# A decoder layer in fp32 on one core: the first entry's order written out on four engines, the identity made first, loads reordered, and the experts' sums taken in another order

## The chip, the core and the metric

One core of a Trainium2 chip runs the whole layer as one program. The metric is the time of the program on the device in microseconds, as a median of several executions. A core has five engines with a queue of instructions each: PE (TensorE, matrix products and transposes), DVE (VectorE), ACT (ScalarE), POOL (GpSimd) and SP (SyncE, which here only issues DMAs). ACT and POOL issue DMAs too. An engine takes its queue in order, so an instruction that waits holds up all that stands behind it.

## The reference

What is computed, cut to what matters (16 entries of 128 tokens, 256 wide):

```python
x = x + attn(layernorm(x))             # 16 heads of 64, self-attention within an entry
x = x + xattn(layernorm(x), ctx, mask) # 16 heads of 16, keys and values from ctx, keys masked
x = x + ffn(layernorm(x))              # all 8 experts, 256 -> 512 -> 256, exact gelu, summed,
                                       # times norm_g = g / (g + 1e-6) of the top gate
...
logits = xf @ gate_w.T + gate_b
logits = logits * rsqrt(mean(logits ** 2) + eps) * rms_w
g = softmax(logits / 0.5).max(-1)
```

Every expert's output counts for every token; the gate only gives the factor.

## The kernel before, in words

**Loads** (lines 130 to 198). SP and ACT issue the big loads, POOL the small ones: the row constants `rowv` broadcast to all partitions, the mask `msk`, and eight column pieces `bqk2`. SP starts with the first entry's tokens and shares the four quarters of `wq` and `wk` with ACT; ACT then issues the two halves of `wv`, SP the tokens of entries 1 to 3 in one load, the first context, the cross-attention's weights `wx` (in small pieces) and `wx_vo`, the remaining tokens, `wo`, and the experts' first weights. A load's landing is told by one of eight semaphores in turn, so a ninth load is issued when the first has landed.

**The identity** (lines 201 and 202) is written by POOL, two operations; PE's transposes multiply by it.

**The entry of token block 0** (lines 786 to 825). Statistics and inverse root on DVE (`deviations`, lines 250 to 291), the normalized tokens `xn` (295), two transposes on PE (304), a copy by ACT to `xnT` (246 or 234, both are helpers through which many operations pass), keys and queries (378, four columns of heads per call: `keys(0, 0)`, `queries(0, 0)`, ...), values (417), then the same normalization for block 1. Around it stand preparations: the scaled bias `bk1` (205), the statistics of blocks 2 and 3, `hidden_keys` from the mask (803), `masked`, `par` and `bkp` (805 to 819) for the cross-attention, and two cleared tiles `v2` (824). In this stretch only PE's order is that of the code; the order on DVE, ACT and POOL is chosen by a scheduler when the program is built.

**The slots** (lines 737 to 784, 827 to 835). After the entry, 16 slots run, one per entry, in which self-attention of entry s, cross-attention of s-1 and s-2, the expert norm of s-3 and the projections of s+1 are woven together. Each step has a due time in the table `DUE` (in us of a slot of 28.2); `at` puts it in a heap, `run_slots` takes the steps out in order of due time, and that order holds on PE, DVE, ACT and POOL. Slot 0 starts with the scores S0 and S1 (433). Then follow the largest value per row `nmax` (319), exponentials (325, ACT), reciprocals `rinv` (336), the product with them on POOL (340), transposes `tr_p` (355), their copies `prT` by DVE, the products `po` with the values (457), `atT`, and the output product `mm_o` (477), which reads `wo`. Twelve late statistics `st0` to `st11` are spread over slot 0.

**The experts** (lines 982 to 1121). Four blocks of 512 tokens; the products of 2x2 blocks are done with seven products in place of eight. For each of 16 pairs p of hidden blocks: four products into the banks ha, hb, hf, he (`hidden_first`), three more added into ha, hf, he (`hidden_last`), gelu on ACT, and seven products into sums 1 to 7 (`summed`). The sums lie two to a PSUM bank in the order `ORDER = (2, 3, 4, 8, 1, 7, 5, 6)`, so the banks hold (2, 3), (4, 8), (1, 7) and (5, 6). At the end of a token block `finished` combines the sums: ACT copies sum 1 to `u[0]`, DVE adds (1036 to 1042) and writes `yT` with the bias (`plus`, 1032). While the next block runs its pairs 0 and 1 this goes on; after pair 1, `rest` transposes yT on PE (eight transposes, banks hb and hf), DVE multiplies by the gate and adds the tokens (`ot`, 1055), and SP stores. Here only PE's order is written; ACT's and DVE's is the scheduler's.

Of the kernel before, what the change touches and what calls it, by code (L numbers as in the profile page):

```python
# [18 lines left out]
P = 128  # L19
# [7 lines left out]
C2 = 2  # L27
# [37 lines left out]
    cmul1b=27.42, lg=27.6, xn3=27.77, cke=28.26, ab2=28.44, st0=14.3, st1=14.8, st2=15.6,  # L65
    st3=16.2, st4=17.4, st5=17.9, st6=18.4, st7=18.9, st8=20.0, st9=20.5, st10=21.0, st11=21.5,
    late=31.7,
# [6 lines left out]
def decoder_layer(  # L74
# [21 lines left out]

    const = ctx.enter_context(tc.tile_pool(name="const", bufs=1))
# [21 lines left out]


# [16 lines left out]
    for n in range(4):  # L137
        for w, src, q in ((wq, wq1, nc.sync), (wk, wk1, nc.scalar)):
            f = slice(n * 256, (n + 1) * 256)
            q.dma_start(out=w[:, :, f], in_=src[:, :, f])  # L140
    for n in range(2):
        f = slice(n * 512, (n + 1) * 512)
        nc.scalar.dma_start(out=wv[:, :, f], in_=wv1[:, :, f])
    load_tokens(1, 3)
# [21 lines left out]
    wx_vo = wx_p.tile([P, 2, KD, D], F32, tag="wx_vo", name="wx_vo")  # L166
    for n, w in ((1, wk2), (0, wq2)):
        for k in range(KD):
            nc.sync.dma_start(
                out=wx[:, n, k].rearrange("p (h d) -> p h d", d=DH2),  # L170
                in_=w[:, k].rearrange("p (h s) -> p h s", s=32)[:, :, :DH2],
            )
    nc.sync.dma_start(out=wx_vo[:, 0], in_=wv2)
# [27 lines left out]
    ident = const.tile([P, P], F32, tag="ident", name="ident")  # L201
    make_identity(nc, ident)

    bk1 = const.tile([P, C1], F32, tag="bk1", name="bk1")
    nc.vector.tensor_scalar_mul(bk1, colv[:, BK1 : BK1 + C1], DH1 ** -0.5)
# [531 lines left out]
    def slot(s):  # L737
# [38 lines left out]
        if s == 0:  # L776
            mv = variances(B - 4)
# [8 lines left out]
    with tc.manual_schedule(engines={mybir.EngineType.PE}):  # L786
        first = deviations([0])
        self_norm(0)
        add_bias(0, BO1)
        self_norm_transposed(0)  # L790
        first.update(deviations([1]))
        self_norm(1)
        add_bias(1, BO1)
        for n in range(2):
            keys(0, n)
            queries(0, n)
        values(0, 0)
        self_norm_transposed(1)
        values(0, 1)
        first.update(deviations([2, 3]))  # L800

        hidden_keys = const.tile([P, T], U8, tag="hidden_keys", name="hidden_keys")
        nc.vector.tensor_scalar(hidden_keys, msk, 0, None, ALU.is_equal)
        masked = const.tile([P, 1], F32, tag="masked", name="masked")
        nc.vector.memset(masked, MASKED)


        par = const.tile([P, 2], F32, tag="par", name="par")
        bkp = const.tile([P, 2, C2], F32, tag="bkp", name="bkp")
# [11 lines left out]
        v2s = []  # L821
        for i in range(2):
            v2 = wx_p.tile([P, GB, 2 * VW], F32, tag=f"v2_{i}", name=f"v2_{i}")
            nc.gpsimd.memset(v2, 0.0)
            v2s.append(v2)

    with tc.manual_schedule(
        engines={
            mybir.EngineType.PE,
            mybir.EngineType.DVE,  # L830
            mybir.EngineType.Activation,
            mybir.EngineType.Pool,
        }
    ):
        run_slots(B)
# [190 lines left out]
    def finished(m, sums, plain):  # L1026
# [7 lines left out]
        nc.scalar.copy(u[:, 0], ys[1])  # L1034
        plus(yT[:, 0, :HT], 0, ys[2], u[:, 0])
        nc.vector.tensor_add(u[:, 1], u[:, 0], ys[6])
        nc.vector.tensor_add(u[:, 3], u[:, 1], ys[5])
        plus(yT[:, 0, HT:], 0, ys[3], u[:, 3])
        nc.vector.tensor_add(u[:, 2], u[:, 1], ys[7])  # L1039
        plus(yT[:, 1, :HT], 1, ys[4], u[:, 2])  # L1040
        if plain:
            nc.vector.tensor_add(u[:, 2], u[:, 2], ys[8])
        plus(yT[:, 1, HT:], 1, ys[5], u[:, 2])

        def rest():
            for i in range(MT // P // 2):
                tr = ps_h.tile([P, 4, P], F32, tag=("hb", "hf")[i], name="tr_y")
                for j in range(2):
                    for k in range(KD):
                        t0 = (2 * i + j) * P  # L1050
                        nc.tensor.transpose(tr[:, 2 * j + k, :], yT[:, k, t0 : t0 + P], ident)
                ot = rp.tile([P, 2, D], F32, tag="ot", name="ot")
                b0 = m * (MT // P) + 2 * i
                for j in range(2):
                    nc.vector.scalar_tensor_tensor(
                        ot[:, j, :],
                        tr[:, 2 * j : 2 * j + 2, :].rearrange("p k t -> p (k t)"),
                        gn[:, b0 + j : b0 + j + 1],
                        xs[:, b0 + j, :],
                        ALU.mult,  # L1060
                        ALU.add,
                    )
                nc.sync.dma_start(
                    out=out[b0 : b0 + 2].rearrange("b t d -> t b d"), in_=ot
                )

# [13 lines left out]
    def experts():  # L1080
# [12 lines left out]
        for m in range(NT // MT):  # L1093
            for p in range(0 if m else PRE, NP):
# [20 lines left out]
                if p == 1 and rest is not None:  # L1115
                    rest()
                    rest = None
# [71 lines left out]
```

## Time and profile before

| what | us |
|---|---|
| median of 3 executions (lowest, highest) | 886.25 (886.09, 886.84) |
| the profiled execution, its span | 886.86, 884.9 |
| PE busy in the span | 860.6 |
| first transpose, first product of keys, first scores | 12.72, 14.79, 28.69 |
| start of the scores of slots 1, 2, 3 | 51.40, 75.57, 103.36 |
| joints of the experts' token blocks (first product of the next block's sums) | 584.13, 683.75, 783.41 |
| last product of the sums, last store issued | 877.50, 881.81 |

Times count from the start of the span. A row of the timeline has start, duration, engine, line, operation, what it writes `<-` what it reads, how many were merged, and in brackets how long the engine had been idle and what ended that. A row of the waits has the engine and line that waited, for whom, the total, the number of times and the longest.

### The profile page before, as it was taken

Reading aid. Unit: us, or ns where it says so; the run is one execution under the profiler, and the core shown is the slowest. Engines: PE = TensorE matmul, PEld = TensorE weight load, DVE = VectorE, ACT = ScalarE, POOL = GpSimd, SP = SyncE. Lnnn points to the kernel's source line nnn. Section 1 sums busy time; section 2 is a strip of 40 time slices with the busy share of each in tenths; the row PEclk is TensorE's granted clock in tenths of the full one; section 3 lists DMA queues with packets and bytes.
Section 4 is the critical chain, followed back from the end, with each engine's and each line's share of the span. In section 5 each row is a group of like instructions: output and inputs, shape, how many; then the busy total and the mean of one; then the engine's idle time right before and its main releaser. Section 6 shows DMA issues by size and latency. Waiting matters only on the chain.

```text
span 884.9 us, 16050 instructions
## 1 busy us (share of the span) xinstructions
PE 860.6 (97%) x5984; PEld 721.3 (82%) x5984; DVE 626.4 (71%) x1528; ACT 425.8 (48%) x1622; POOL 166.3 (19%) x178
## 2 busy tenths in 40 slices
PE   3999999999999999999999999999999999999997
PEld 3788888888888888888876558878888888878886
DVE  3687877778777877778776489675657666575655
ACT  1457655675557655675544804333333333333332
POOL 3224232342334232342322100000000000000000
PEclk9999999999999999999999999999999999999999
DMA  9700000000000000000051010000000000000000
GB/s 211 258 1 13 2 2 13 1 13 1 1 14 1 14 1 1 14 1 1 2 183 56 1 49 0 1 24 1 1 0 1 25 1 1 0 24 1 1 1 24
DMA packets 19262, 21.30 MB, mean 24 GB/s; under 512 B 9504, under 2 KB 15664, under 8 KB 18544
## 3 DMA queue, kind: packets, MB, share of 16 engines
q1 hardware_dynamic: 17040, 17.84, 6.4%
q10 hardware_dynamic: 1776, 2.14, 0.9%
q8 instruction: 47, 0.77, 0.4%
q0 software_dynamic: 368, 0.30, 0.3%
q14 instruction: 31, 0.25, 0.1%
HBM read 18.16 MB, written 2.10 MB: 23 GB/s over the span
## 4 chain that ended last, share of the span: by engine, by line
PE 91%; DVE 5%; ACT 1%; DMA 1%; issue 1%; POOL 0%; SPq 0%; ACTq 0%; DVEq 0%; POOLq 0%
PE y L980 18%; PE mm_qk L378 13%; PE mm_v L417 6%; PE tr_p L355 6%; PE mm_o L477 6%; PE hf L980 5%; PE he L980 5%; PE ha L980 5%; PE sc L433 3%; PE po L457 3%; PE y L867 3%; PE hb L980 3%; PE mm_h L727 3%; PE sc L567 2%; PE po L606 2%; PE mm_k L494 2%
## 5 line engine op out<-in xcount | busy, mean ns | idle before, releaser
L340 POOL TENSOR_TENSOR cpr<-cpr,rinv 128x512 f32<-128x512 f32 x64 | 68.5, 1070 | 221.5 <-DVE rinv L336 221.1
L325 ACT ACTIVATE cpr<-sc,nmax 128x128 f32<-128x128 f32 x256 | 89.7, 411 | 11.6 <-DVE nmax L319 11.6
L325 ACT ACTIVATE pr<-sc,nmax 128x128 f32<-128x128 f32 x256 | 90.6, 419 | 1.8 <-DVE nmax L319 1.8
L319 DVE TENSOR_REDUCE nmax<-sc 128x8 f32<-128x1024 f32 x64 | 76.7, 1219 | 10.7 <-PE sc L433 10.7
L340 POOL TENSOR_TENSOR pr<-pr,rinv 128x512 f32<-128x512 f32 x64 | 65.9, 1041 | 80.8 <-DVE rinv L336 80.8
L1010 DVE TENSOR_TENSOR c<-u,hf 128x256 f32<-128x256 f32 x56 | 23.6, 421 | 71.7 <-PE hf L980 71.6
L1009 ACT ACTIVATE h<-u,colv 128x256 f32<-128x256 f32 x56 | 28.4, 507 | 91.9 <-DVE u L996 90.2
L378 PEld LDWEIGHTS mm_qk<-xnT,wk 128*128 128x128 f32 x512 | 62.5, 196 | 8.9 <-issue 4.3
L246 ACT COPY xnT<-tr_x 128x256 f32<-128x256 f32 x42 | 15.6, 372 | 109.9 <-PE tr_x L304 109.9
L980 PE MATMUL hf<-xt,w 128*128 128x256 f32 x224 | 67.1, 381 | 0.3
L980 PE MATMUL ha<-xnT,w 128*128 128x256 f32 x224 | 66.6, 379 | 0.0
L980 PE MATMUL y<-t,w 128*128 128x256 f32 x224 | 66.6, 379 | 0.0
L325 ACT ACTIVATION_READ_ACCUMULATOR pr<-sc,nmax 128x1 f32 x256 | 66.3, 259 | 0.0
L378 PE MATMUL mm_qk<-xnT,wk 128*128 128x128 f32 x512 | 64.2, 280 | 1.4 <-ACT xnT L234 1.4
L378 PE MATMUL mm_qk<-xnT,wq 128*128 128x128 f32 x512 | 65.1, 281 | 0.0
L325 ACT ACTIVATION_READ_ACCUMULATOR cpr<-sc,nmax 128x1 f32 x256 | 64.4, 252 | 0.0
L378 PEld LDWEIGHTS mm_qk<-xnT,wq 128*128 128x128 f32 x512 | 61.1, 195 | 3.0 <-issue 2.9
L993 ACT COPY u<-ha 128x256 f32<-128x256 f32 x56 | 20.8, 372 | 87.1 <-PE ha L980 87.1
L417 PE MATMUL mm_v<-wv,xnT 128*128 128x512 f32 x128 | 60.2, 592 | 0.0
L980 PE MATMUL y<-h,w 128*128 128x256 f32 x224 | 57.7, 380 | 1.4 <-DVE yu L1039 1.4
L477 PE MATMUL mm_o<-wo,atT 128*128 128x256 f32 x256 | 57.9, 379 | 0.0
L246 DVE COPY prT<-tr_p 128x512 f32<-128x512 f32 x64 | 39.8, 684 | 19.4 <-PE tr_p L355 19.3
(164 smaller groups left out, 1880.2 us busy)
## 6 DMA issues: line engine op xcount, KB each, us to landing
w<-in_w SPq DMA_DIRECT2D x8, 1024.0 KB, 5.4
ctx<-in_ctxT SPq DMA_DIRECT2D x8, 256.0 KB, 2.7
out_x<-ot SPq DMA_DIRECT2D x8, 256.0 KB, 2.2
xs<-in_x SPq DMA_DIRECT2D x3, 512.0 KB, 7.0
wk<-in_wk ACTq DMA_DIRECT2D x4, 256.0 KB, 9.2
wq<-in_wq SPq DMA_DIRECT2D x4, 256.0 KB, 10.6
wv<-in_wv ACTq DMA_DIRECT2D x2, 512.0 KB, 7.9
wo<-in_wo SPq DMA_DIRECT2D x1, 1024.0 KB, 9.9
```

The lines of the kernel that those rows point to most:

```text
L246: f(*a)
L319: nc.vector.tensor_reduce(w["nmax"], sc, AX.X, ALU.max, negate=True)
L325: nc.scalar.activation(w["pr"][:, i, :], sc[:, i, :], AF.Exp, bias=w["nmax"][:, i : i + 1], scale=1.0, accum_out=sums[:, j : j + 1],)
L340: nc.gpsimd.tensor_tensor(four, four, w["rinv", n].unsqueeze(2).broadcast_to([P, 4, T]), ALU.mult)
L355: nc.tensor.transpose(tr[:, j, :], w["pr"][:, 4 * n + j, :], ident)
L378: nc.tensor.matmul(mm[:, i, :], w[:, k, c * P : (c + 1) * P], xnT1[:, k, 0, :], start=(k == 0), stop=(k == KD - 1),)
L417: nc.tensor.matmul(mm, entry["xnT1", b][:, k, 0, :], wv[:, k, f], start=(k == 0), stop=(k == KD - 1),)
L433: nc.tensor.matmul(sc[:, j, c * T : (c + 1) * T], qT[r, 4 * half + c, :], kT[r, 4 * half + c, :], start=True, stop=True,)
L457: nc.tensor.matmul(po[j * DH1 : (j + 1) * DH1, c, :], v[:, h * DH1 : (h + 1) * DH1], prT[:, 4 * j + c, :], start=True, stop=True,)
L477: nc.tensor.matmul(mm[:, :D], atT[:, c, :], wo[:, c, :], start=(c == 0), stop=(c == C1 - 1))
L980: nc.tensor.matmul(out, left[p // q][n - 1][:, p % q], rights[n - 1], **flags)
L1009: nc.scalar.activation(h[:, 1, 1], u[:, 3], AF.Gelu, bias=col(B1 + 2 * p + 1))
```

## The change

- One written order for PE, DVE, ACT and POOL from the beginning of the program to the end of the slots, in place of PE's alone in the entry.
- The identity is made ahead of all loads.
- Loads: wv's halves go from ACT's queue to SP's, behind the tokens of entry 1, which are loaded alone; the cross-attention's value weights (`wx_vo[:, 0]`) and the tokens of entries 2 and 3 go ahead of `wx`.
- `bk1` stands behind the first normalization; the statistics of block 1 stand behind the first keys and queries; those of blocks 2 and 3 become steps of slot 0 (due 6.65, 6.7 and 7.9), and the masks' and biases' preparation becomes a step of slot 0 (`cross`, due 13.9). The cleared tiles v2 go ahead of the entry.
- Experts: `finished` adds in another order (`u[2]` right after `u[1]`, all three ahead of the outputs; the two outputs of the second half exchanged where `plain` is not set); `rest` is done in two portions, after pairs 1 and 2, both through the bank he; the last pair's products come in the order 1, 5, 7, 6, 2, 3, 4.

```diff
-    cmul1b=27.42, lg=27.6, xn3=27.77, cke=28.26, ab2=28.44, st0=14.3, st1=14.8, st2=15.6,
+    cmul1b=27.42, lg=27.6, xn3=27.77, cke=28.26, ab2=28.44, early0=6.65, early1=6.7, early=7.9,
+    cross=13.9, st0=14.3, st1=14.8, st2=15.6, st3=16.2, st4=17.4, st5=17.9, st6=18.4, st7=18.9,
...
+    in_order = ExitStack()
+    in_order.enter_context(
+        tc.manual_schedule(
+            engines={
+                mybir.EngineType.PE,
+                mybir.EngineType.DVE,
+                mybir.EngineType.Activation,
+                mybir.EngineType.Pool,
+            }
+        )
+    )
...
+    ident = const.tile([P, P], F32, tag="ident", name="ident")
+    make_identity(nc, ident)
...
+    load_tokens(1, 1)
     for n in range(2):
         f = slice(n * 512, (n + 1) * 512)
-        nc.scalar.dma_start(out=wv[:, :, f], in_=wv1[:, :, f])
-    load_tokens(1, 3)
+        nc.sync.dma_start(out=wv[:, :, f], in_=wv1[:, :, f])
...
+    nc.sync.dma_start(out=wx_vo[:, 0], in_=wv2)
+    load_tokens(2, 2)
     for n, w in ((1, wk2), (0, wq2)):
...
-    nc.sync.dma_start(out=wx_vo[:, 0], in_=wv2)
...
-    ident = const.tile([P, P], F32, tag="ident", name="ident")
-    make_identity(nc, ident)
...
-    nc.vector.tensor_scalar_mul(bk1, colv[:, BK1 : BK1 + C1], DH1 ** -0.5)
...
         if s == 0:
+            mv2 = variances(2)
+            for i in range(2):
+                at(f"early{i}", statistics, mv2[:, i, :], 2 + i)
+            at("early", lambda: first.update(inverse_deviations(mv2, [2, 3])))
+            at("cross", for_cross)
...
+    first = deviations([0])
+    self_norm(0)
+    add_bias(0, BO1)
+    self_norm_transposed(0)
+
+    nc.vector.tensor_scalar_mul(bk1, colv[:, BK1 : BK1 + C1], DH1 ** -0.5)
+    keys(0, 0)
+    queries(0, 0)
+    first.update(deviations([1]))
+    self_norm(1)
+    add_bias(1, BO1)
+    keys(0, 1)
+    queries(0, 1)
+    values(0, 0)
+    self_norm_transposed(1)
+    values(0, 1)
...
         nc.scalar.copy(u[:, 0], ys[1])
+        nc.vector.tensor_add(u[:, 1], u[:, 0], ys[6])
+        nc.vector.tensor_add(u[:, 2], u[:, 1], ys[7])
+        nc.vector.tensor_add(u[:, 3], u[:, 1], ys[5])
         plus(yT[:, 0, :HT], 0, ys[2], u[:, 0])
-        nc.vector.tensor_add(u[:, 1], u[:, 0], ys[6])
-        nc.vector.tensor_add(u[:, 3], u[:, 1], ys[5])
         plus(yT[:, 0, HT:], 0, ys[3], u[:, 3])
-        nc.vector.tensor_add(u[:, 2], u[:, 1], ys[7])
-        plus(yT[:, 1, :HT], 1, ys[4], u[:, 2])
         if plain:
+            plus(yT[:, 1, :HT], 1, ys[4], u[:, 2])
             nc.vector.tensor_add(u[:, 2], u[:, 2], ys[8])
-        plus(yT[:, 1, HT:], 1, ys[5], u[:, 2])
+            plus(yT[:, 1, HT:], 1, ys[5], u[:, 2])
+        else:
+            plus(yT[:, 1, HT:], 1, ys[5], u[:, 2])
+            plus(yT[:, 1, :HT], 1, ys[4], u[:, 2])
...
-                tr = ps_h.tile([P, 4, P], F32, tag=("hb", "hf")[i], name="tr_y")
+            tr = ps_h.tile([P, 4, P], F32, tag=bank, name="tr_y")
...
-                if p == 1 and rest is not None:
-                    rest()
-                    rest = None
+                if p in (1, 2) and rest is not None:
+                    rest(p - 1, "he")
                 before = now
-        summed((1, 2, 3), *before, ys)
-        summed((7, 5, 6, 4), *before, ys)
-        finished(m, ys, False)()
+        summed((1, 5, 7, 6, 2, 3, 4), *before, ys)
+        rest = finished(m, ys, False)
+        for i, bank in enumerate(("hb", "hf")):
+            rest(i, bank)
```

The function `for_cross` holds what stood at lines 803 to 819, unchanged.

More of the change, by code (lines that the diff above doesn't have):

```diff
@@ L64 @@
     root=24.79, k1=25.19, ve1=25.39, gate=26.93, ke1=27.13, cr1b=27.14, ck=27.19, xn=27.27,
-    cmul1b=27.42, lg=27.6, xn3=27.77, cke=28.26, ab2=28.44, st0=14.3, st1=14.8, st2=15.6,
-    st3=16.2, st4=17.4, st5=17.9, st6=18.4, st7=18.9, st8=20.0, st9=20.5, st10=21.0, st11=21.5,
-    late=31.7,
+    cmul1b=27.42, lg=27.6, xn3=27.77, cke=28.26, ab2=28.44, early0=6.65, early1=6.7, early=7.9,
+    cross=13.9, st0=14.3, st1=14.8, st2=15.6, st3=16.2, st4=17.4, st5=17.9, st6=18.4, st7=18.9,
+    st8=20.0, st9=20.5, st10=21.0, st11=21.5, late=31.7,
 )
@@ L784, in slot, with for_cross @@
             at("late", rest)
[L786 to L802, printed above, removed]
+    v2s = []
+    for i in range(2):
+        v2 = wx_p.tile([P, GB, 2 * VW], F32, tag=f"v2_{i}", name=f"v2_{i}")
+        nc.gpsimd.memset(v2, 0.0)
+        v2s.append(v2)
+    first = deviations([0])
[13 more added lines that the diff above has]
+    values(0, 1)
+    hidden_keys = const.tile([P, T], U8, tag="hidden_keys", name="hidden_keys")
+    masked = const.tile([P, 1], F32, tag="masked", name="masked")
+    par = const.tile([P, 2], F32, tag="par", name="par")
+    bkp = const.tile([P, 2, C2], F32, tag="bkp", name="bkp")
+    def for_cross():
         nc.vector.tensor_scalar(hidden_keys, msk, 0, None, ALU.is_equal)
-        masked = const.tile([P, 1], F32, tag="masked", name="masked")
         nc.vector.memset(masked, MASKED)
-        par = const.tile([P, 2], F32, tag="par", name="par")
-        bkp = const.tile([P, 2, C2], F32, tag="bkp", name="bkp")
         for e in range(2):
@@ L819, in decoder_layer @@
             nc.vector.tensor_scalar_mul(bkp[:, e, :], bqk2[:, 1, :], par[:, e : e + 1])
[L821 to L835, printed above, removed]
+    run_slots(B)
+    in_order.close()
     alone.close()
@@ L1041, in finished @@
         if plain:
+            plus(yT[:, 1, :HT], 1, ys[4], u[:, 2])
             nc.vector.tensor_add(u[:, 2], u[:, 2], ys[8])
-        plus(yT[:, 1, HT:], 1, ys[5], u[:, 2])
-        def rest():
-            for i in range(MT // P // 2):
-                tr = ps_h.tile([P, 4, P], F32, tag=("hb", "hf")[i], name="tr_y")
[L1048 to L1064, printed above, removed]
+            plus(yT[:, 1, HT:], 1, ys[5], u[:, 2])
+        else:
+            plus(yT[:, 1, HT:], 1, ys[5], u[:, 2])
+            plus(yT[:, 1, :HT], 1, ys[4], u[:, 2])
@@ new lines, in rest @@
+        def rest(i, bank):
+            tr = ps_h.tile([P, 4, P], F32, tag=bank, name="tr_y")
+            for j in range(2):
+                for k in range(KD):
+                    t0 = (2 * i + j) * P
+                    nc.tensor.transpose(tr[:, 2 * j + k, :], yT[:, k, t0 : t0 + P], ident)
+            ot = rp.tile([P, 2, D], F32, tag="ot", name="ot")
+            b0 = m * (MT // P) + 2 * i
+            for j in range(2):
+                nc.vector.scalar_tensor_tensor(
+                    ot[:, j, :],
+                    tr[:, 2 * j : 2 * j + 2, :].rearrange("p k t -> p (k t)"),
+                    gn[:, b0 + j : b0 + j + 1],
+                    xs[:, b0 + j, :],
+                    ALU.mult,
+                    ALU.add,
@@ L1065, in rest @@
                 )
+            nc.sync.dma_start(out=out[b0 : b0 + 2].rearrange("b t d -> t b d"), in_=ot)
         return rest
```

## The prediction

> **What bounds the kernel now.** I read the page first, then who TensorE (PE) waited for, then the timeline of the stages that the diff touches. The page:
>
> ```profile
> PE 860.6 (97%) x5984; PEld 721.3 (82%) x5984; DVE 626.4 (71%) x1528; ACT 425.8 (48%) x1622; POOL 166.3 (19%) x178
> PE 91%; DVE 5%; ACT 1%; DMA 1%; issue 1%; POOL 0%; SPq 0%; ACTq 0%; DVEq 0%; POOLq 0%
> ```
>
> PE is busy for 97% of the span and 91% of the chain that ended last is PE. The change takes no arithmetic away, so it can only gain where PE stands still. PE's waits, longest first (total, times, longest):
>
> ```profile
> PE tr_x L304 <- POOL ident masks.py:199: 12.7, 1, 12.7
> PE tr_y L1051 <- DVE yT L1032: 1.5, 1, 1.5
> PE hb L980 <- DVE ot L1055: 1.5, 3, 0.5
> PE y L980 <- DVE yu L1039: 1.4, 3, 0.5
> PE mm_qk L378 <- ACT xnT L234: 1.4, 1, 1.4
> ```
>
> The first and the last are the entry, about 14 us; the three in between are the three joints of the experts' token blocks and the tail, about 4 us. So the entry decides. Its timeline:
>
> ```profile
> 1.27 0.74 POOL L145 DMA_DIRECT2D rowv<-in_rows  x1 [0.82 <-POOLq L1177]
> ...
> 4.16 0.15 DVE L255 TENSOR_SCALAR root_t<-var 128x1 int32<-128x1 int32 x1
> ...
> 9.16 3.87 ACTq L143 DMA_DIRECT2D wv<-in_wv  x2
> ...
> 9.54 0.23 DVE L803 TENSOR_SCALAR hidden_keys<-msk 128x128 uint8<-128x128 uint8 x1 [5.23 <-DMA msk<-in_mask]
> ...
> 11.21 0.41 DVE L295 TENSOR_SCALAR xn<-xs,mv,root 128x256 f32<-128x256 f32 x1
> ...
> 12.38 0.29 POOL masks.py:199 TENSOR_SCALAR_AFFINE_SELECT ident<-ident 128x128 f32<-128x128 f32 x1
> ...
> 13.07 1.28 ACT L234 ACT_TABLE_LOAD   x1 [13.07 <-DMA wk<-in_wk]
> 14.36 0.37 ACT L234 COPY xnT<-tr_x 128x256 f32<-128x256 f32 x1
> ...
> 14.79 3.78 PE L378 MATMUL mm_qk<-xnT,wk 128*128 128x128 f32 x16 [1.37 <-ACT xnT L234]
> ```
>
> The reader is to see three queues blocked by something that the first product does not need: DVE stands 5.23 us behind hidden_keys, which waits for the mask; POOL writes the identity behind its own loads; ACT issues the two halves of wv (each issue waits for an earlier load) before its table load and the copy.
>
> **1. The entry.** In the built order of the changed kernel hidden_keys is gone from before xn, the identity is POOL's first work, and ACT issues only colv and wk.
> - DVE: after root_t (end 4.31) the rest of the chain, 9.69 to 11.62 in the trace, is 1.93 us: xn ends at 6.3.
> - POOL: free at 1.27; 0.22 and 0.29 us of row time, and at most the 1.08 us that POOL idled between them: identity by 2.9. Hidden behind xn; without that cover it would cost what passes 6.3.
> - PE's two transposes take 0.69 us: 7.1. ACT is through with its issues at 4.55, the table load ends near 5.9, the copy takes 0.37: 7.5.
> - The first product also needs the first quarter of wk. By its issue (1.19) and landing time (8.0 us) that landed at 9.2; the other quarters, in the same way: wk 10.0, 12.6, 14.2; wq 9.3, 12.4, 13.9, 14.9.
>
> So the first product starts between 7.5 (data early) and 9.2 (data as before). What held the data? Columns here: stretch, busy per engine, clock, share of DMA time, GB/s.
>
> ```profile
> 4.00:6.00 2.00, 0.00 (x0) 0.00 (x0) 0.28 (x2) 0.00 (x0) 2.00 (x4) 1.00 0.75 153
> 6.00:8.00 2.00, 0.00 (x0) 0.00 (x0) 0.00 (x0) 0.00 (x0) 0.21 (x1) 1.00 1.03 336
> ```
>
> Until rowv has landed (1.27 + 6.9 = 8.2) the rate is half of what it is afterwards. rowv is now issued 0.5 to 1.6 us later, behind the identity, so some of wk and wq gets past it. I take the middle, **8.3: 6.5 us earlier** than 14.79 (ends 5.6 and 7.3).
>
> From there I move the old sequence as it is. Eight matmuls of a quarter take 8 x 0.213 = 1.7 us at first, so the quarters are wanted at 8.3, 10.0, 11.7, 13.4 and on, no earlier than they landed. wv is wanted at 8.3 + 10.15 = 18.5 and 20.4; it landed at 17.8 and 19.6 with 384 KB of tokens beside it, and now has 128 KB ahead of it. The context and wv2 are wanted at 24.2 and come right after wv, 512 KB, 1.7 us at 300 GB/s. SP's queue also carries tokens 2 and 3 ahead of wx now: first used in slot 0, near 28. wo is wanted near 37.8 and landed at 35.2, with the same bytes ahead of it: 2.6 us of cover.
>
> The clock: mm_qk starts are 0.213 us apart until 20.9 and 0.112 after, 6.1 us from the first product, though the clock column says 1.00. I keep that stretch as long as it was.
>
> [...]
>
> **2. What moves into slot 0.** DVE had the roots of tokens 2 and 3 and the masks' constants behind it before the scores; now they stand in slot 0. In the trace's own times:
>
> ```profile
> 35.76 0.18 DVE L336 RECIPROCAL rinv<-sums 128x4 f32<-128x4 f32 x1 [1.22 <-ACT pr L325]
> ...
> 37.16 0.18 DVE L336 RECIPROCAL rinv<-sums 128x4 f32<-128x4 f32 x1 [1.22 <-ACT pr L325]
> 37.25 0.38 DVE L295 TENSOR_SCALAR xn<-xs,mv,root 128x256 f32<-128x256 f32 x1
> 37.41 1.12 POOL L340 TENSOR_TENSOR pr<-pr,rinv 128x512 f32<-128x512 f32 x1 [0.36 <-DVE rinv L336]
> 37.57 2.68 DVE L246 COPY prT<-tr_p 128x512 f32<-128x512 f32 x4
> ```
>
> The four statistics (1.1 us, as the pair at 40.17 to 41.25) fit in the idle before 35.76. The twelve root operations do not: the same twelve for 12 columns run from 54.80 to 57.15, 2.3 us. They stand between the third and the fourth reciprocal, so the fourth goes from 37.16 to 38.2, the fourth product on POOL ends at 39.5 instead of 38.53, and the four prT copies end near 41.1 instead of 40.25. PE's second po group starts right after them (40.48): **0.9 us later**. Queued behind it on DVE are the masks' constants (about 1.2 us) and the late statistics; atT then ends at 44.0 and 45.7, wanted at 44.3 and 46.0: covered, by 0.3 us. In slot 1 nmax starts 0.4 later than PE's own shift, which that slot's transposes just absorb. Ends: 0.3 (POOL's product was late only by the overlap) and 1.8 (the cover of 0.3 is gone in slots 0 and 1).
>
> **3. The joints, three times.** Before:
>
> ```profile
> 584.13 1.10 PE L980 MATMUL y<-h,w 128*128 128x256 f32 x4 [0.52 <-DVE yu L1039]
> ...
> 589.74 1.65 DVE L1055 SCALAR_TENSOR_TENSOR ot<-tr_y,gn,xs 128x256 f32<-128x256 f32 x4
> ...
> 590.76 0.67 PE L980 MATMUL hb<-xt,k 128*128 128x256 f32 x2 [0.49 <-DVE ot L1055]
> ```
>
> - Transposes in two portions. PE's products come 0.43 us apart; hb came at 590.76 instead of 590.1 and hf then at 591.54 instead of 591.19: 1.0 us lost. Now four transposes stand ahead of ha, and the bank is he, wanted as the fourth product, near 590.53; two ot end at 590.6. About 0.23 us lost, twice: 0.55 saved per joint, **1.6 us** in three (ends 0.6 and 2.4).
> - Order of the sums. Product 1 wants the bank of sums 1 and 7, freed by yu (L1039): a place earlier now, 0.33 us. But in the built DVE order (left to the scheduler) another yT stands ahead of the one that frees the bank of sums 2 and 3; that ends at 584.8 instead of 584.4, and product 2 starts at 584.93 instead of 584.56. So 0.37 us is lost per joint, of which the first gets 0.18 back at he, where PE waited for DVE anyway: **+0.9 us** (ends -1.0, if the bank comes free in time, and +1.1).
>
> **4. The tail.** Sum 7 is the third product instead of the fourth, so the copy of sum 1 starts 0.43 earlier (876.25). But DVE then has three yu and four yT in a row: 876.68 + 0.46 + 0.33 + 0.33 + 3 x 0.42 + 0.48 = 879.54, where the yT that PE waited for ended at 879.46. **+0.1** (ends -0.4, +0.4).
>
> **Sum.** -6.5 + 0.9 - 1.6 + 0.9 + 0.1 = -6.2. The profiled execution took 886.86 with a span of 884.9, 2.0 around it: 878.7 + 2.0 = **880.7**. Its own time is 0.6 above the median of the three (886.25, from 886.09 to 886.84), the high end of them.
>
> **Rivals.**
> - The data set the start (25%): wk lands at 9.2 as before, and the slot-0 loss is at its upper end. -5.6 + 1.8 - 0.6 = -4.4, or **882.5**. For it: landing times show no slack below 9.2. Against: rowv is out of the way at first.
> - The data come early (17%): start at 7.5, and the bank of sums 2 and 3 is free in time. -7.3 + 0.9 - 1.6 - 1.0 + 0.1 = -8.9, **878.0**.
> - wv goes through one queue instead of two (5%): both queues were in use until wv landed, and if SP's queue alone is slower, wv, the context and wo slide. values(0,0) would wait; with the gain cut to within 1.7 us, about **885.5**. Against: SP alone carries 254 to 415 GB/s from 24 to 38.
> - wo is too late, and slower than before (3%): the output product of slot 0 stands behind it. It costs from a landing at 37.8 on; from 44 the whole gain is gone, from 46 it is slower: at 48, **888.7**. It would have to land 13 us later than it did with the same bytes ahead, hence the small chance.
>
> Forecast 50%. Faster by over 0.2% (1.77 us, about what a measurement of this kernel can tell from no change): 50 + 25 + 17 = 92%; within 5%; slower 3%. The range leaves out the last two and the outer half of the early case: 878.2 to 883.6.
>
> **What would show it.** PE's wait for the identity is gone and tr_x starts near 6.4; the first mm_qk starts at 7.5 to 9.2 and waits for a load; the first sc starts near 22.2 instead of 28.69; a PE gap of about a microsecond appears at tr_p or po in slot 0; hb's wait is gone and he waits 0.2 us six times; y at the joints waits for yT rather than yu. I am wrong if the first mm_qk starts after 10, if mm_v or mm_o waits for a load, or if slots 1 to 3 take longer than before.

## The result

The changed kernel takes **879.6 us** (median of 6 executions, 878.69 to 882.39); the kernel before, run beside it, 886.17 us (6 executions, 885.25 to 886.84). The ratio is 0.9928, with a 95% interval from 0.9913 to 0.9944. A second series later, on another chip, gave 880.31 us (5 executions, 879.63 to 882.20) against 886.02 us, ratio 0.9945 [0.9932, 0.9959]. Forecast: 880.7, range 878.2 to 883.6.

The profiled execution of the changed kernel took 879.95 us, its span is 878.2. Its page, the same two lines as before (busy time of the engines, and the chain that ended last):

```profile
PE 859.7 (98%) x5984; PEld 719.8 (82%) x5984; DVE 626.4 (71%) x1528; ACT 426.1 (49%) x1622; POOL 166.6 (19%) x178
...
PE 92%; DVE 4%; issue 1%; DMA 1%; ACT 1%; POOL 0%; DVEq 0%; ACTq 0%; POOLq 0%
```

The instructions are as many as before, 5984 matmuls and 1528 operations of DVE, and DVE's busy time is the same; PE's is 0.9 us less, although it does the same products. That 0.9 is a first hint that the clock had a part in it. What PE waited for (total, times, longest):

```profile
PE tr_x L315 <- DVE bk L814: 6.2, 1, 6.2
PE mm_qk L389 <- DMA wk<-in_wk: 1.9, 1, 1.9
PE tr_p L366 <- POOL pr L351: 1.5, 1, 1.5
PE tr_y L1066 <- DVE yT L1045: 1.3, 2, 0.8
PE y L993 <- DVE yT L1045: 1.2, 3, 0.4
...
PE he L993 <- DVE u L1009: 0.2, 1, 0.2
```

Of the five waits of before, hb's is gone and the first is half as long. The first product waits for a load now. The third row is new: 1.5 us in slot 0 for a product of POOL. The entry, from the timeline:

```profile
1.02 0.29 POOL masks.py:199 TENSOR_SCALAR_AFFINE_SELECT ident<-ident 128x128 f32<-128x128 f32 x1
...
1.46 0.74 POOL L159 DMA_DIRECT2D rowv<-in_rows  x1 [0.15 <-issue]
...
4.27 1.28 ACT L245 ACT_TABLE_LOAD   x1 [4.27 <-issue]
...
5.65 0.41 DVE L306 TENSOR_SCALAR xn<-xs,mv,root 128x256 f32<-128x256 f32 x1
...
6.21 0.66 PE L315 MATMUL tr_x<-ident,xn 128*128 128x128 f32 x2 [6.21 <-DVE bk L814]
6.90 0.37 ACT L245 COPY xnT<-tr_x 128x256 f32<-128x256 f32 x1 [1.35 <-PE tr_x L315]
...
8.76 0.55 PE L389 MATMUL mm_qk<-xnT,wk 128*128 128x128 f32 x1 [1.90 <-DMA wk<-in_wk]
```

The identity is ready at 1.3, xn at 6.1, the copy at 7.3; then PE stands 1.90 us until the first quarter of wk is there. (The first row of the waits names `bk`, which follows xn on DVE; the transposes wait for xn.)

The two profiled executions, mark by mark, in us from the start of the span:

| mark | before | after | gained so far |
|---|---|---|---|
| first transpose | 12.72 | 6.21 | 6.5 |
| first product of keys | 14.79 | 8.76 | 6.02 |
| first scores (slot 0) | 28.69 | 21.29 | 7.40 |
| scores of slot 1 | 51.33 | 45.59 | 5.74 |
| scores of slot 3 | 103.29 | 97.67 | 5.62 |
| first product of the experts | 526.33 | 520.47 | 5.86 |
| last product of the sums | 877.51 | 870.40 | 7.11 |
| end of the span | 884.88 | 878.18 | 6.70 |

So 6.02 come from the start, 1.38 more until the scores, 1.66 are lost in slot 0, 1.25 come back at the joints, and 0.41 is lost after the last product.

### The profile page after: what moved, and what is told of

Same layout as the page of the kernel before. It is cut to its first block, busy times and chain, and to the rows that moved or that the text cites. A ratio compares the mean times of both kernels' runs of the same rounds, so it can differ in the third digit from the quotient of the medians.

```text
span 878.2 us, 16053 instructions
## 1 busy us (share of the span) xinstructions
PE 859.7 (98%) x5984; PEld 719.8 (82%) x5984; DVE 626.4 (71%) x1528; ACT 426.1 (49%) x1622; POOL 166.6 (19%) x178
## 4 chain that ended last, share of the span: by engine, by line
PE 92%; DVE 4%; issue 1%; DMA 1%; ACT 1%; POOL 0%; DVEq 0%; ACTq 0%; POOLq 0%
PE y L993 18%; PE mm_qk L389 13%; PE mm_v L428 6%; PE tr_p L366 6%; PE mm_o L488 6%; PE he L993 5%; PE hf L993 5%; PE ha L993 5%; PE sc L444 4%; PE po L468 3%; PE y L880 3%; PE mm_h L738 3%; PE hb L993 3%; PE sc L578 2%; PE po L617 2%; PE mm_k L505 2%
```

## The experiments

Twelve experiments. Each starts from the changed kernel; times of a single execution are so marked. The span marks are those of the table above. Experiments 1 to 4 ran on one chip, 5 to 8 on another, 9 to 12 on a third, each beside the kernel before (medians 885.49, 885.68 and 886.02 us), so small differences are read from stretches of a profile and not from the whole time.

**1. wv back on ACT's queue.**

```diff
-        nc.sync.dma_start(out=wv[:, :, f], in_=wv1[:, :, f])
+        nc.scalar.dma_start(out=wv[:, :, f], in_=wv1[:, :, f])
```

> The changed kernel with one of its three repairs undone: wv's two loads are issued by ACT again, behind wk. Theory (each of the three queues held the start by itself): ACT's two issues wait for earlier loads and end near 10.3 us, the table load (1.28) and the copy (0.37) follow, so the first mm_qk starts near 12.1 instead of 8.76, and the time is 3.3 us longer. Rival (the other two repairs carry the gain, and ACT's queue was in nobody's way): first mm_qk within 0.5 us of 8.76.

Measured (one execution): 888.19 us, span 886.3. The first product starts at 14.12, later than even the theory had it, for ACT's two issues lasted longer. The timeline of ACT, and the product:

```profile
8.16 4.21 ACTq L158 DMA_DIRECT2D wv<-in_wv  x2
12.40 1.28 ACT L245 ACT_TABLE_LOAD   x1 [12.40 <-DMA wk<-in_wk]
13.70 0.37 ACT L245 COPY xnT<-tr_x 128x256 f32<-128x256 f32 x1
...
14.12 1.22 PE L389 MATMUL mm_qk<-xnT,wk 128*128 128x128 f32 x4 [7.26 <-ACT xnT L245]
```

This one line of the change undone takes back 5.36 of the 6.02 us. The time is 2.7 us above the kernel before beside it, although only the start was touched: against the changed kernel the span is 8.1 us longer, of which 5.36 come from the first product, 1.2 from the stretch up to the scores and 1.6 from slot 0. The last two are a matter of the clock (below).

**2. The identity behind POOL's loads again.**

```diff
-    ident = const.tile([P, P], F32, tag="ident", name="ident")
-    make_identity(nc, ident)
...
+    ident = const.tile([P, P], F32, tag="ident", name="ident")
+    make_identity(nc, ident)
     bk1 = const.tile([P, C1], F32, tag="bk1", name="bk1")
```

> The changed kernel with the identity behind POOL's own loads again. Theory: POOL comes to it near 10.8 us, it is done near 11.4, transposes 0.66, copy 0.37: first mm_qk near 12.5, 3.7 us later than in the changed kernel, and as much longer in time. Rival: no loss over 0.5 us.

Measured (one execution): 883.17 us. Identity written from 9.67 to 10.26, first transpose 10.32, first product 11.47: 2.7 us later, a microsecond less than the theory said.

```profile
9.97 0.29 POOL masks.py:199 TENSOR_SCALAR_AFFINE_SELECT ident<-ident 128x128 f32<-128x128 f32 x1
...
10.32 0.69 PE L315 MATMUL tr_x<-ident,xn 128*128 128x128 f32 x2 [10.32 <-POOL ident masks.py:199]
```

**3. hidden_keys ahead of the first normalization again.**

```diff
+    nc.vector.tensor_scalar(hidden_keys, msk, 0, None, ALU.is_equal)
     first = deviations([0])
```

> The changed kernel with hidden_keys ahead of the first statistics on DVE. Theory: DVE stands until the mask has landed (near 10.2 us), then its chain of 3.0 us, transposes and copy follow: first mm_qk near 14.6, 5.9 us later than in the changed kernel. Rival: no loss over 0.5 us, because the data were what the start waited for.

Measured (one execution): 884.75 us. hidden_keys at 9.43, first transpose 12.72, first product 13.84: 5.1 us later, 0.8 less than the theory said.

```profile
9.43 0.23 DVE L810 TENSOR_SCALAR hidden_keys<-msk 128x128 uint8<-128x128 uint8 x1 [6.04 <-DMA msk<-in_mask]
```

The three parts undone one at a time cost 5.4, 2.7 and 5.1 us, 13.2 together, where all together brought 6.0. They lie side by side on three engines: ACT's queue or DVE's alone holds PE nearly as long as all three, the identity alone for less than half of it.

**4. The roots of tokens 2 and 3 back in the entry**, and their load ahead of the context.

```diff
-            at("early", lambda: first.update(inverse_deviations(mv2, [2, 3])))
...
     values(0, 1)
+    first.update(deviations([2, 3]))
```

> The changed kernel with the statistics and roots of tokens 2 and 3 taken out of slot 0 and put at the end of the entry, and their load put ahead of the first context. Theory (the roots in slot 0 cost PE its gap of 1.5 us at tr_p): tokens 2 and 3 land near 18.5 us, the roots end near 22, before the first nmax at 22.5; the gap at tr_p goes to under 0.3, slot 0 (scores to scores of slot 1) goes from 24.3 to 22.7 us, and the time is 1.3 to 1.6 us shorter than that of the changed kernel (879.6), so 878.0 to 878.3. Rival (the gap comes from POOL's or ACT's own pace there, which was there before in small): the gap stays over 1 us and the time is the same within 0.3.

Measured: median 878.96 us (4 executions, 878.25 to 879.87), ratio to before 0.9920 [0.9904, 0.9937]. The theory's 878.0 to 878.3 us is missed by 0.7, and a gain over the changed kernel (ratio 0.9928) is not shown by the whole times. The slot shows it: slot 0 lasts 22.59 us instead of 24.30 (before: 22.64). In its stretch the waits of PE hold only

```profile
PE tr_p L366 <- ACT kT L415: 0.3, 1, 0.3
```

The 1.5 us for POOL's product are gone. The roots ended at 23.33 and not near 22, still 0.6 us ahead of the first nmax (23.95). The scores start 1.45 us later than in the changed kernel; the clock came up at 14.96, 6.10 us behind the first product instead of 3.27, and half of that difference is 1.4.

**5. The roots one place earlier in slot 0**: `early=7.8` instead of 7.9.

> The roots of token tiles 2 and 3 stand one place earlier in slot 0: ahead of the third reciprocal instead of behind it; nothing else differs from the changed kernel. [...] Slot 0 24.3 us long, to 0.3. [...]

What it is to tell apart is seen in the changed kernel's slot 0: whether the 1.05 us of one operation come from POOL's product beside it or from the operation's own form.

```profile
28.47 0.14 DVE L294 TENSOR_SCALAR var<-mv 128x2 f32<-128x2 f32 x1
...
28.63 1.04 POOL L351 TENSOR_TENSOR pr<-pr,rinv 128x512 f32<-128x512 f32 x1 [0.36 <-DVE var L294]
28.64 1.05 DVE L266 TENSOR_SCALAR root_t<-var 128x2 int32<-128x2 int32 x1
...
29.73 0.17 DVE L267 TENSOR_SCALAR root<-root_t 128x2 int32<-128x2 int32 x1
...
31.57 0.17 DVE L347 RECIPROCAL rinv<-sums 128x4 f32<-128x4 f32 x1
...
31.82 1.18 POOL L351 TENSOR_TENSOR pr<-pr,rinv 128x512 f32<-128x512 f32 x1 [2.15 <-DVE rinv L347]
...
33.06 0.66 PE L366 MATMUL tr_p<-ident,pr 128*128 128x128 f32 x4 [1.51 <-POOL pr L351]
```

One operation on two columns takes 1.05 us, and it begins and ends with POOL's product beside it. In experiment 5, one place earlier:

```profile
26.72 1.04 POOL L351 TENSOR_TENSOR pr<-pr,rinv 128x512 f32<-128x512 f32 x1 [0.63 <-DVE rinv L347]
...
27.74 0.17 DVE L294 TENSOR_SCALAR var<-mv 128x2 f32<-128x2 f32 x1
...
27.94 0.17 DVE L266 TENSOR_SCALAR root_t<-var 128x2 int32<-128x2 int32 x1
...
31.48 0.66 PE L366 MATMUL tr_p<-ident,pr 128*128 128x128 f32 x4 [1.41 <-POOL pr L351]
```

POOL's product ends at 27.76, the same operation of the same shape stands behind it and takes 0.17 us. So the 1.05 come from the neighbour on POOL and not from the operation's form. Slot 0 lasts 24.22 us and the gap stays (1.41 and 0.34), since two reciprocals are late now: 879.34 us (one execution). The slot is as long as was expected.

All ten traces in which the operation stands at this place have 1.05 us, beside a product of 1.04 in the changed kernel. But not every operation lasts that long: in the kernel before, a `tensor_scalar` on one column took 0.15 us in the middle of such a product (rows at 73.50 and 73.69 below). What tells the two cases apart was not shown.

**6. PE kept busy from the start.** 28 transposes that nobody reads.

```diff
+    busy(20)
     first = deviations([0])
     self_norm(0)
...
     self_norm_transposed(0)
+    busy(8)
```

> Twenty transposes of the identity into a spare bank of TensorE are added ahead of the first tr_x and eight behind it; nobody reads what they write. Nothing else differs from the changed kernel. Theory (the slow stretch is counted from TensorE's first busy stretch, in windows of about 3.4 us whose phase is chance; the changed kernel's short stretch of 3.3 us was luck): the clock is full when, or less than 1 us after, the first mm_qk starts at 8.8; the products then follow the quarters of wk and wq as they land, the scores of slot 0 start at 20.3 to 20.6 instead of 21.3 and 22.7, and the median is 1 to 2 us below the changed kernel's 879.6, near 878, with a smaller spread. Rival (the stretch is tied to the first real products or to their data): the products are as slow as before, the scores start at 21.3 to 24, and the time is 879 to 881.

Measured: median 879.36 us (4 executions: 878.63, 878.67, 880.05, 880.38), ratio to before 0.9928 [0.9912, 0.9945]. In the profiled execution:

```profile
1.36 4.46 PE L813 MATMUL warm<-ident 128*128 128x128 f32 x20 [1.36 <-POOL ident masks.py:199]
6.07 0.44 PE L315 MATMUL tr_x<-ident,xn 128*128 128x128 f32 x2 [0.25 <-DVE xn L306]
6.35 1.04 PE L813 MATMUL warm<-ident 128*128 128x128 f32 x8
8.30 0.91 PE L389 MATMUL mm_qk<-xnT,wk 128*128 128x128 f32 x6 [0.91 <-DMA wk<-in_wk]
```

The 20 transposes run at about 0.22 us each, the 8 behind them at half of that: the clock came up near their end (5.63), before the first product, and the scores start at 19.97 instead of 21.29. This half of the theory holds, though 0.46 of the 1.32 us come from the first product, whose quarter of wk landed at 8.16 instead of 8.63. The other half, a smaller spread and a median near 878, does not: two of the four executions are about 1.4 us or more above the others, and the median lies where the rival had it (879 to 881). The next experiments show a cause in slot 0.

**7. The rest of a token block at one point again**, behind pair 1, through hb and hf; the order of the sums stays new.

```diff
-                if p in (1, 2) and rest is not None:
-                    rest(p - 1, "he")
+                if p == 1 and rest is not None:
+                    for i, bank in enumerate(("hb", "hf")):
+                        rest(i, bank)
+                    rest = None
```

> The rest of the block before is transposed at one point, behind pair 1, in the banks hb and hf, as in the kernel before; the sums keep their new order. Theory (the portions through he are worth the wait for hb and hf, 0.49 and 0.11 a joint, less the two waits of 0.06): hb and hf wait again, 0.5 to 0.6 us a joint, three joints, 1.4 to 1.6 us later at the last y than the changed kernel measured from the first experts' product. Rival (the products behind the joint absorb it): under 0.5 us in all.

Measured (one execution): 883.36 us. From the experts' first product to the last y 351.36 us instead of 349.93: **1.43 us** for the two portions. The wait is back:

```profile
PE hb L993 <- DVE ot L1070: 1.5, 3, 0.5
```

That accounts for 1.4 of the 3.4 us by which this execution was slower than the changed kernel's. Of the others, 0.5 were there at the first scores (21.76), and 1.6 came in slot 0, which nothing in the edit touches. The stretches of the profile show it (stretch, its length, busy time of PE, PEld, DVE, ACT, POOL, then PE's granted clock, share of DMA time, GB/s):

```profile
30.31:33.72 3.41, 1.56 (x13) 1.12 (x12) 3.10 (x15) 1.40 (x5) 1.44 (x2) 1.00 1.02 415
33.72:37.13 3.41, 3.41 (x28) 3.08 (x28) 3.10 (x14) 0.37 (x1) 0.43 (x1) 0.50 1.04 410
```

PE was granted half its clock for 3.41 us, right behind a stretch of 3.41 us in which it had been busy for 1.56. Experiment 1 had the same (half from 40.38 to 43.79), and so had experiments 9 and 10 below.

**8. The order of the sums, and of the last pairs, as before**; the two portions stay.

```diff
-        summed((1, 5, 7, 6, 2, 3, 4), *before, ys)
+        summed((1, 2, 3, 7, 5, 6, 4), *before, ys)
...
+        plus(yT[:, 0, :HT], 0, ys[2], u[:, 0])
         nc.vector.tensor_add(u[:, 1], u[:, 0], ys[6])
-        nc.vector.tensor_add(u[:, 2], u[:, 1], ys[7])
         nc.vector.tensor_add(u[:, 3], u[:, 1], ys[5])
...
```

> The order of the sums, of the last pairs and of the kernel's end as before; the rest in two portions as in the changed kernel. Theory (the new order moves a wait from yu to yT and is worth 0.0 to 0.2 us a joint, and costs 0.4 us in the tail): experts from the first product to the last y 0.0 to 0.5 us longer than in the changed kernel, the tail 0.3 to 0.5 us shorter, the sum within 0.3 us. Rival (my forecast: the order costs 0.3 us a joint and 0.1 in the tail): joints 0.9 us shorter in all, the sum 1.0 us shorter.

Measured (one execution): 879.13 us. Experts from first product to last y 349.73 us, 0.20 **shorter** than with the new order (nine other traces with the changed kernel's experts have 349.92 to 349.96); from the last y to the last store issued 4.30 us in both. So the new order costs 0.07 us a joint and brings nothing in the tail. The theory's bounds on the joints (0.0 to 0.5 longer) missed by 0.2, its tail was wrong: the tail did not get shorter. My forecast's 0.3 a joint was four times too much.

**9. The end in another order.**

```diff
-        summed((1, 5, 7, 6, 2, 3, 4), *before, ys)
+        summed((1, 7, 5, 6, 4, 2, 3), *before, ys)
...
+                plus(yT[:, 1, HT:], 1, ys[5], u[:, 2])
+                plus(yT[:, 1, :HT], 1, ys[4], u[:, 2])
+                plus(yT[:, 0, :HT], 0, ys[2], u[:, 0])
+                plus(yT[:, 0, HT:], 0, ys[3], u[:, 3])
```

> Only the last token block differs from the changed kernel: its sums come in the order 1, 7, 5, 6, 4, 2, 3, and VectorE's four yT are written out as yT11, yT10, yT00, yT01, so that both halves of the first two token tiles are there before the second two. Theory (in the tail the first ot waits for the fourth yT only because of their order): from the last y to the first ot 2.15 us instead of 2.61, and the last output is issued 0.4 to 0.5 us earlier; the closing waits of SyncE stay as they are (0.49 us behind the last output's). Rival (VectorE's seven operations in a row set the end, whatever their order): 2.6 us again, within 0.1.

Measured (one execution): 881.65 us, with the clock halved in slot 0 (from 33.54, 3.41 us). From the last y to the first ot 2.33 us instead of 2.61, to the last store issued 4.02 instead of 4.30: 0.28 gained where the theory had 0.4 to 0.5.

```profile
872.65 1.65 DVE L1045 SCALAR_TENSOR_TENSOR yT<-y,b,yu 128x256 f32<-128x256 f32 x4
873.97 0.86 PEld L1076 LDWEIGHTS tr_y<-ident,yT 128*128 128x128 f32 x8 [1.66 <-DVE yT L1045]
873.97 1.09 PE L1076 MATMUL tr_y<-ident,yT 128*128 128x128 f32 x8 [1.26 <-DVE yT L1045]
874.66 1.66 DVE L1080 SCALAR_TENSOR_TENSOR ot<-tr_y,gn,xs 128x256 f32<-128x256 f32 x4 [0.36 <-PE tr_y L1076]
```

The transposes start at the third yT, as meant. But DVE, done with its fourth, then stands 0.36 us for the transposes, where the theory had it go on at once.

**10. One load less.**

```diff
-    for b0 in range(4, B, 4):
-        load_tokens(b0, 4)
+    load_tokens(4, 4)
+    load_tokens(8, 8)
```

> Token tiles 8 to 15 are loaded by one transfer instead of two, late in the entry; nothing else differs from the changed kernel. The change had added one load (48 on SyncE's and ScalarE's queues before, 49 after), and SyncE's closing waits stood in another order: the wait for the last output third of ten, with seven behind it, where it was the last of ten before. Theory (the eight semaphores of the loads are used in turn, and the closing waits go through them in a fixed order, so that one load fewer turns the last output's wait back to the end): from the issue of the last output to the span's end 3.06 us as in the kernel before, instead of 3.48; 0.42 us gained. Rival (the closing order has another cause): 3.48 us again.

Measured (one execution): 882.05 us, again with the clock halved in slot 0 (34.92 to 38.33). From the issue of the last store to the end of the span 3.07 us, as in the kernel before (3.06), instead of 3.48. SyncE's closing waits, in us after that issue:

| wait number | 1 | 2 | 3 | 4 | 5 | 6 | 7 | 8 | 9 | 10 | end of span |
|---|---|---|---|---|---|---|---|---|---|---|---|
| before | .42 | .48 | .54 | .61 | .67 | .73 | .79 | .85 | 1.41 | **2.17** | 3.06 |
| after | .42 | .48 | **2.16** | 2.22 | 2.28 | 2.34 | 2.40 | 2.46 | 2.52 | 2.58 | 3.48 |
| one load less | .42 | .48 | .54 | .61 | .67 | .73 | .79 | .85 | 1.40 | **2.17** | 3.07 |

The bold one waits for the last store, 2.16 us after its issue in all three. In the kernel before, with 48 loads and stores on SP's and ACT's queues, the trace has eight semaphores that transfers raise 96 times each, 16 times by each transfer; the last store is told by the eighth, and its wait is the last of ten. In the changed kernel, with 49, the first is raised 112 times: the turn has moved on by one, the last store is told by the first, and seven waits of 0.06 us that were long satisfied stand behind it: 0.42 us. The change made one load into two (tokens 1 to 3), so this is its doing.

**11. Four edits together**: experiments 4, 6, 9 and 10.

> The changed kernel with four edits together: the roots of token tiles 2 and 3 back in the entry, TensorE kept busy on transposes of the identity that nobody reads until the first product, the last block's order of the sums and of yT, and one load less. Theory (the four terms add up): scores of slot 0 at 20.0, slot 0 22.6 us long instead of 24.3, the tail 0.4 shorter by the order and 0.4 by the closing waits, and no window of TensorE idle enough to lower the clock, so that the runs lie within 1 us of each other: median 876.2, between 875.6 and 876.8. Rival (the gains overlap: what the entry gains is lost to loads that are now late, or the clock is still chance): 877.5 or more, with a spread over 1.5 us.

Measured: median **876.99 us** (4 executions, 876.67 to 877.45), ratio to before 0.9901 [0.9887, 0.9914]; 3.3 us less than the changed kernel on the same chip. The spread, 0.8 us, is what the theory said; the median is 0.8 above it. Two places: the scores start at 20.40 instead of 20.0 (the first quarter of wk landed at 8.46, and at 8.16 in experiment 6; why was not tried), and slot 0 lasts 23.34 instead of 22.6, of which 0.55 stand at the output product:

```profile
35.73 1.53 PE L488 MATMUL mm_o<-wo,atT 128*128 128x256 f32 x6 [0.39 <-DVE st L287]
```

The named releaser had ended; wo, issued at 25.58, takes 10.0 us to land in this kernel (8.7 in the changed one, issued at 25.71), which is 35.6. So wo is late now, as one of my rivals had it for the change itself: the work ahead of it has become faster, and a load of twice the size stands before it. That the larger load is the cause is not shown: wo took 10.1 us in experiment 10, which has it too, but 9.7 in experiment 6 and 11.2 in experiment 1, which have not.

**12. The changed kernel once more**, beside experiment 11.

> The changed kernel itself, once more, beside the kernel with four edits. Theory (two things of chance move it: the slow stretch behind the first product, 2.7 to 6.1 us long, worth up to 1.7 us; and whether the two gaps of slot 0, 1.87 us together, fall into one window of 3.41 us, which costs another 1.6 us of clock): median 879.6, to 0.6, single runs between 878.5 and 882.5, and at most one run in three above 881. Rival (the runs differ for reasons of the chip, not of the kernel): the same spread in the kernel with four edits.

Measured: 879.63, 880.08, 880.31, 881.72 and 882.20 us, median 880.31. Two of five above 881, where I had at most one in three; the median 0.1 outside. But the rival does not hold: the kernel with four edits, on the same chip at the same time, spreads over 0.8 us, this one over 2.6. The spread is the kernel's.

**Why it spreads.** In each profiled execution with a halved clock, the half lasts 3.41 us and starts a whole multiple of 3.413 us after the clock first came up. The clock's fall at the end keeps the same step: it was full from 20.92 to 881.08 us in the kernel before and from 12.03 to 875.61 in the changed one, 860.16 and 863.57 us, which are 252 and 253 times 3.413. So I cut each execution into windows of 3.413 us from that moment, and took PE's idle time in the one with the gaps of slot 0 (0.35 for kT and 1.5 for POOL's product):

| profiled execution | PE idle in that window of 3.41 us | next window |
|---|---|---|
| exp. 3, exp. 8, after, exp. 5, exp. 6, exp. 12 | 1.03, 1.21, 1.32, 1.41, 1.57, 1.66 | full clock |
| exp. 2 | 1.77 | full clock |
| exp. 10, 7, 1, 9 | 1.84, 1.85, 1.86, 1.86 | **half clock** |

In these eleven executions the full clock followed windows with up to 1.77 us of idle, the half those with 1.84 us and more. The end of the kernel agrees: in all fourteen traces the clock dropped right after the first window there with 1.84 us of idle or more (2.43 in the changed kernel, 2.10 in the kernel before), and stayed up after windows with up to 1.39. Both gaps of slot 0 together are 1.86 us and reach over 2.49 us, so they fall into one window when it begins within the 3.41 - 2.49 = 0.92 us that this leaves: 27% of executions, by estimate, each 1.6 us longer (slot 0 25.9 instead of 24.3). The kernel before has 0.31 us of idle there and never comes near.

Executions without a trace have a mean granted clock on record. In the fourteen traces a halved window goes with 0.996 or 0.997, none with 0.998 or more. Of the changed kernel's eleven executions, the three above 881 us (881.72, 882.20, 882.39) have 0.996 and the other eight 0.998 or 0.999; in experiment 6 the two longer ones (880.05, 880.38) have 0.996, the others 0.998; experiment 11 has 0.999 to 1.000. So these three had the halved clock too, and three of eleven agrees with the estimate, as far as eleven executions can tell.

The same windows set the slow stretch behind the first product, here from that product to the moment the clock came up:

| execution | idle in the window of the first product, us | slow stretch, us |
|---|---|---|
| after, exp. 8, 3, 5 | 0.14, 0.35, 0.46, 0.50 | 3.27, 3.06, 2.76, 2.91 |
| before, exp. 4, 10 | 0.69, 0.73, 0.81 | 6.13, 6.10, 6.02 |
| exp. 1, 7, 9, 2, 12 | 1.05, 1.60, 1.69, 1.97, 2.23 | 5.77, 4.69, 4.47, 4.16, 3.93 |

In the executions with up to 0.50 us idle in that window the clock came up at its end; in those with 0.69 or more it came up at the end of the next. The windows begin at another moment of the kernel in each execution (0.14 us ahead of the first product in the changed kernel, 0.70 in the kernel before), as by chance.

## Why the prediction was right, point by point

The time lay 1.1 us under the forecast and inside the range, in the case I held likeliest; the first product at 8.76 is between the forecast's 8.3 and the first rival's 9.2. That the sum came so close is in part luck: the entry, slot 0 and the tail brought 1.5 us less than forecast, and the slow stretch, the joints and slots 1 to 15 brought 2.0 more. By terms, as the profiled executions have them:

| term | forecast | measured | shown by |
|---|---|---|---|
| entry, to the first product | -6.5 | -6.02 | exp. 1, 2, 3 |
| the slow stretch | 0 | -1.38 | chance of the window |
| slot 0 | +0.9 | +1.66 | exp. 4, 5 |
| slots 1 to 15 | 0 | -0.12 | - |
| joints: two portions | -1.6 | -1.43 | exp. 7 |
| joints: order of the sums | +0.9 | +0.20 | exp. 8 |
| tail | +0.1 | +0.41 | exp. 10 |
| sum | -6.2 | -6.70 | |

- **The entry: right.** All three queues had to be cleared, each of them holds PE alone (experiments 1 to 3), and when they were, the data set the start. The transposes started at 6.21 (forecast 6.4), the copy ended at 7.27 (7.5). I took the middle between "data early" and "data as before"; wk landed at 8.63, 0.5 before its old time (9.14). rowv was issued only 0.19 us later than before, not the 0.5 to 1.6 that I counted with, for the identity took less time on POOL than I allowed. And my reason for the middle, that wk gets past a later rowv, is not borne out: in experiment 2 rowv was issued at 1.27 as in the kernel before, and wk landed at 8.41. In the thirteen traces other than before's it landed between 8.07 and 8.73; what brought it forward stays open.
- **The slow stretch: kept equal, and it was not.** 6.13 us before, 3.27 after. Over the twelve profiled executions without extra transposes (both kernels and experiments 1 to 5, 7 to 10 and 12) it ranges from 2.76 to 6.13 us, by where a window happens to begin. So 1.4 us of this pair's difference belong to these two executions, and are not shown to be a property of the change. The medians of the two series differ by 6.57 and 5.71 us.
- **Slot 0: the mechanism right, the term half of what it was.** I saw the twelve root operations between the third and the fourth reciprocal, and priced them at 0.195 us each, from rows (54.80 to 57.15) beside which POOL was idle. In slot 0 the third reciprocal starts POOL's product, and the second root operation runs into it: 0.90 us more. 0.9 + 0.9 = 1.8 is close to the measured 1.66, and equal to the upper end that I gave for another reason. The fourth reciprocal came 10.28 us behind the first scores, and 8.47 in the kernel before: 1.81 later. The rows that told it were in the trace of before: at 21.02 a root operation took 0.72 us beside an operation of POOL of 0.72, and at 73.88 another took 0.68 beside one of 1.04, where 0.16 to 0.22 is their time alone. Not every one took longer: the two int32 operations at 73.50 and 73.69 took 0.15 beside the same product.

```profile
21.00 0.72 POOL L308 TENSOR_TENSOR xs<-xs,rowv 128x256 f32<-128x256 f32 x1 [8.33 <-DVE root L268]
21.02 0.72 DVE L266 TENSOR_TENSOR root_t<-root 128x2 f32<-128x2 f32 x1
...
73.50 0.15 DVE L255 TENSOR_SCALAR root_t<-var 128x1 int32<-128x1 int32 x1
73.50 1.04 POOL L340 TENSOR_TENSOR cpr<-cpr,rinv 128x512 f32<-128x512 f32 x1 [0.35 <-DVE var L283]
73.69 0.15 DVE L256 TENSOR_SCALAR root<-root_t 128x1 int32<-128x1 int32 x1
73.88 0.68 DVE L264 SCALAR_TENSOR_TENSOR root_t<-root,var 128x1 f32<-128x1 f32 x1
```

- **And slot 0 has a second price that I had not seen**: with the 0.35 us that PE lost there anyway the gap comes to 1.86 us, and in experiments 1 and 7 cost 1.6 us of clock.
- **The joints.** The portions gave what was forecast; he waits 0.06 us each time, not 0.23. The order of the sums costs a fifth of what I had. There the step that failed is: "So 0.37 us is lost per joint, of which the first gets 0.18 back at he". Product 1 came 0.33 earlier (its wait fell from 0.52, 0.45 and 0.45 to 0.18, 0.12 and 0.12), and product 2 waits 0.45, 0.36 and 0.36, both as said. But the later two joints get the loss back too: in the second joint of the kernel before, the matmuls of hf and he stood 0.35, 0.32 and 0.31 apart at three places, where 0.215 is their pace, that is 0.33 us of small waits for DVE; afterwards one of 0.26 is left. From product 1 to tr_y it is 4.72 us before and 5.06 after there, so nothing is lost on balance, and 4.67 and 5.20 in the first joint, so 0.2.
- **The tail: +0.41 where I had +0.1, and the place wrong.** From the last y to the last store, which my +0.1 was about, the two kernels agree to 0.01 us (4.31 and 4.30). The 0.41 us lie behind it, in SyncE's closing waits, which I had not looked at.
- **The rivals.** That wv, through one queue, would be late did not happen: it landed at 16.3 and 17.7, wanted at 17.5 and 19.5. wo landed at 34.4, in time. Only with four edits together did wo come late, by 0.5 us. (My price for that rival was added up wrongly: a landing at 48 would give 880.7 + 10.2 = 890.9 by its own terms, not 888.7.)
- **The signs of being wrong.** The first product came before 10, and neither mm_v nor mm_o waited for a load. Slots 1 to 3 did take longer than before, by 0.11 us, all of it in slot 1 (24.28 us instead of 24.17), where the forecast had a lateness of 0.4 us just absorbed.

Open: 0.24 us that the experts' first product gained on slot 3's scores (a wait of 0.44 us for cprT became 0.21), in all kernels with the new order; no experiment was aimed at it. Windows of PE with between 1.77 and 1.84 us of idle weren't tried.

## What to carry to other kernels

When several engines each hold up the first product, clear all of their queues together and expect the time that the slowest load allows: undoing any one of three lost 2.7 to 5.4 of the 6.0 us again. When small VectorE operations are moved into a busy stage, price them from a row where GpSimd works beside them, with the same operation and shape, and look for the row whose duration ends with GpSimd's. Gaps in TensorE's work can cost more than their length. Here windows of 3.41 us with 1.84 to 1.86 us of idle (experiments 1, 7, 9 and 10) were followed by half the clock for 3.41 us, 1.6 us lost on top in experiments 1 and 7; with 1.77 (experiment 2) the clock stayed full. So add up the gaps that lie close together, and close one of them: without POOL's gap (experiment 4) slot 0 lasted 22.59 us.

## What the runs showed of the hardware that I had not expected

- The granted clock fell to half for 3.41 us after a window of 3.41 us with 1.84 us of idle (experiment 10), in the middle of dense work; the loss was 1.6 us in experiments 1 and 7.
- Work that nobody reads brought the clock up before the first product (20 transposes from 1.36 us, full clock at 5.63), and the scores started 1.3 us earlier, of which 0.46 are due to an earlier landing.
- A two-column operation on VectorE lasted as long as GpSimd's product beside it: 1.05 us instead of 0.17. A `tensor_scalar` on one column took 0.15 beside such a product.
- The number of loads, by which of eight semaphores the last store is told, moved the end by 0.42 us.
